# Sums of h inside the first scores, rows of W by another queue, and a shorter last store, in a two-layer graph kernel

## The chip, the core and the metric

The kernel runs on one core of a Trainium2 chip. That core has TensorE (PE in the profile, its weight loads PEld), VectorE (DVE), ScalarE (ACT), GpSimd (POOL) and SyncE (SP), and 16 DMA engines that all queues share. The metric is the device time of one launch in microseconds, lower is better. A measurement is the median of three runs.

## What is computed

Two graph layers over 2708 nodes with 1024 features, in float32. Cut to what matters (biases of layer 0 are zero in the inputs, but are computed):

```python
h = max(layernorm(x), 0)                              # layer 0
f, g = h @ Wf + bf, h @ Wg + bg
scores = where(adj > 0, relu(f @ g.T), -9e15)
x = x + softmax(scores, axis=1) @ (h @ W + bW)

h = max(layernorm(x), 0)                              # layer 1
hw = h @ W1
e = leaky_relu(hw @ a1 + (hw @ a2).T, 0.2)
x = x + relu(softmax(where(adj > 0, e, -9e15), axis=1) @ hw)
```

## The kernel before

**Tiling.** The nodes are cut into five panels of columns (512 to 576 wide) and ten pairs of 128-row tiles, numbered 0 to 9, with one more unit for what is left over. Every large product is done as a Strassen-like scheme: seven products, named M1 to M7, of half-size operands, whose sums and differences VectorE makes before and after. The order of the seven is written out by hand for each stage. The stages of layer 0, panel by panel, are: `project_q` (a small product that prepares the right side of the scores), `scores` (L1360), column maxima and softmax, `aggregate` (L892, attention times h), and `project` (L1210, the result times W). Layer 1 has weights, aggregation (by quarters for panels 1 to 4) and projection only.

**Queues.** Nearly all loads go by SP's queue (`load`, L137), in the order in which the program names them: a load that waits for a free buffer keeps the ones behind it waiting. Nearly all stores go by POOL's queue (`store`, L141). Loads use a pool of 12 buffers called `strm` (`stream`, L128), each of 512 KB; a buffer is free again when its last reader has finished, and where it has been stored from, when the store has landed. All accumulation in PSUM uses a pool of eight banks.

**The list of work.** Work on VectorE, ScalarE and POOL that isn't part of a stage is put on a list, `later`, by `put` (L201), each item with an estimated cost in microseconds and perhaps with a `fetch` of its loads. In the loops of matmuls, `behind(us)` (L214) gives the list a credit, at most twice `us`; `one` (L204) takes an item from the front, after it has issued the fetches of the first `ahead[0]` items. An item with `ready` waits at the front until that is true. `ahead` is 5 until the first scores are over, 2 after that, and 1 in the first aggregation.

**Order on VectorE.** A scheduler may move an instruction ahead of others where it thinks that its operands are there. Where `nc.hold` names an engine, its instructions keep the program's order among themselves. `scores` is held so for VectorE (L1408 to L1485).

**The work around the change.** In panel 0 the sums of h for the first aggregation are made from rows that have been stored to `hg_d`. `sums_h` (L365) puts two items for each pair: `first` after a fetch of two tiles called `hr`, and `second` with three stores. They are needed by M5, M6, M7 and M3 of `aggregate(0, 0)`. It is called at L1714, after `scores`, and `sums_until(3)` runs behind the first product of `project_q(1)`, next to `take_max`, which turns `acc` (the running maximum that `scores` leaves) on PE. The loop over pairs in `scores` is L1410 to L1449; what is left over comes after it (L1451 to L1484).

`prepare_W` (L1312) puts eight items of which each loads two blocks of rows of a W, `w_rows`, by `load_rows` (L529), makes four sums and stores them (`right_of_W`, L1189); for layer 1 it makes eight dot products as well (called junk in the profile, after the output that nobody reads). It is called behind M5 of `aggregate(0, 0)`, whose order is M1, M2, M4, M5, M6, M3, M7. `left` (L921) loads the rows of h, called `hc`, for each product. After M3 `inverse_sums` (L865) adds up columns with four matmuls into two banks, takes reciprocals into `rr`, and `scale` (L982) multiplies with them on POOL behind M7.

At the end, `finish1` (L1794) takes each block of the last projection: relu on ScalarE into `o`, an addition to the residual `x_res` on VectorE, and four stores of 32 rows by POOL's queue.

Of the kernel before, what the change touches and what calls it, by code (L numbers as in the profile page):

```python
# [12 lines left out]
OP = mybir.AluOpType  # L13
# [5 lines left out]
P = 128  # L19
# [38 lines left out]
def kernel(  # L58
# [78 lines left out]
    def load(o, i):  # L137
        for a, b in in_16(o, i):
            tc.keep_in_program_order(nc.sync.dma_start(a, b))
# [61 lines left out]
    def put(us, go, fetch=None, takes_psum=False, ready=None, to=later):  # L201
        to.append([us, fetch, go, takes_psum, ready])
# [11 lines left out]
    def behind(us, psum_free=False):  # L214
# [3 lines left out]
        while spare[0] and not later and lazy and credit[0] > 0:  # L218
            credit[0] -= one(lazy)

    def flush():
        while later:
            one()
# [136 lines left out]
        for m, h in ((M1, ha[0]), (M5, ha[1]), (M2, hb[0]), (M4, hb[1])):  # L360
            store(hg_d[i][:, m, j], h)

    summed = [0]

    def sums_h():  # L365

        def fetch(q, two):
            i, j = group_of[q]
            for m in (M1, M2):
                two.append(stream("hr", (P, 2, W)))  # L370
                load(two[-1], hg_d[i][:, m:m + 2, j])

        def first(q, two):
            (a0, a1), (b0, b1) = ((t[:, 0], t[:, 1]) for t in two)
            add(b1, a1, b1)
            sub(a1, a0, a1)

        def second(q, two):
            (a0, a1), (b0, b1) = ((t[:, 0], t[:, 1]) for t in two)
            sub(a0, b1, a0)  # L380
            sub(b0, b0, a0)
            i, j = group_of[q]
            store(hg_d[i][:, M6:M7 + 1, j], two[0])
            store(hg_d[i][:, M3, j], b0)
            store(hg_d[i][:, M5, j], b1)
            summed[0] += 1
        for q in range(NQ):
            two = []
            put(1.4, lambda q=q, two=two: first(q, two), lambda q=q, two=two: fetch(q, two))
            put(1.4, lambda q=q, two=two: second(q, two))  # L390

    BY_QUARTERS = (M1, M5, M2, M6, M7, M3, M4)
    made_quarters = {}
# [132 lines left out]
            one()  # L526


    def load_rows(w, c, name):  # L529
        t = stream(name)  # L530
        load(t, w[c * P:(c + 1) * P, :])
        return t

    wgT, wfT, M, m_left = [None, None], {}, {}, {}

# [356 lines left out]
    def aggregate(l, p, S, sm, then={}, rate=3.0):  # L892
# [89 lines left out]
        def scale():  # L982
            for e, s, k in ((0, slice(0, w), w), (1, hi, h)):
                nc.gpsimd.tensor_tensor(of(e, s), of(e, s), by(s, k), OP.mult)  # L984

        accumulate(left, right, NQ, h, order, then, evict, "g",
                   {**prepare, M3: lambda: inverse.append(inverse_sums(p, sm)), M7: scale}, rate=rate,
                   by_k=True, more={M2: lambda ps: left_over(ps, 0, lo), M3: lambda ps: left_over(ps, 0, hi),
                                    M4: lambda ps: left_over(ps, 1, lo),
                                    (M7, NQ // 2): lambda: (into_m15(), then.get((M7, "middle"), lambda: None)())})  # L990
        nc.vector.tensor_tensor(of(1, lo), of(1, lo), by(lo, h), OP.mult)
        return [t.rearrange("p (c i) -> p c i", c=NH) for t in G]

# [318 lines left out]
    def prepare_W():  # L1312
        ab, rows = [], {}

        def fetch(l, k):
            if l == 1 and not ab:
                for k2, a in enumerate((a1, a2)):
                    row_to_all(a, wab[k2])
                ab.extend(halves(t) for t in wab)
            rows[l, k] = [load_rows(w_in[l], c, "w_rows") for c in (k, k + NH)]  # L1320

        def go(l, k):
            two = rows.pop((l, k))
            if l == 1:
                for i, c in enumerate((k, k + NH)):
                    for j in range(2):
                        dot(wa[:, j, c:c + 1], halves(two[i]), ab[j])
            right_of_W(l, k, *two)

        for l in range(2):  # L1330
            for k in range(NH):
                put(2.7 if l == 0 else 8.0, lambda l=l, k=k: go(l, k), lambda l=l, k=k: fetch(l, k))
# [27 lines left out]
    def scores(p, B):  # L1360
# [9 lines left out]
            row_on_all(rb, r_d[p], p)  # L1370
        acc = slot("acc")
        S = [None] * NT
        rates = (0.6, 1.0, 0.65, 0.65, 0.65)
        lefts = {}

        def product(q, m, ps, start):
# [33 lines left out]
        for q in range(NQ):  # L1410
            n = P
            make_until(q + 2)
            rate = 1.3 if NQ - 1 not in made else rates[p]
            if q + 2 <= LEFT:
                fetch(q + 2)
            if p in ORDERED and q in (2, 6):
                (copy_residual if q == 2 else bias_residual)(p)
            sa, sb = slot("Sa"), slot("Sb")
            S[pairs[q][0]], S[pairs[q][1]] = sa, sb
            X, Y, Z = (bank(f"s{k}") for k in "xyz")  # L1420
            m1, t = slot("sm1"), slot("st")
            product(q, M1, X, True)
            for s in (lo, hi):
                add(m1[:n, s], X[:n, :h], rb[:n, s])
            if left_over:
                left_over()
            product(q, M6, Z, True)
            add(t[:n, lo], Z[:n, :h], m1[:n, hi])
            behind(rate, True)
            product(q, M5, Y, True)  # L1430
            add(t[:n, hi], Y[:n, :h], m1[:n, hi])
            if q + 1 <= LEFT:
                convert(q + 1, p > 0)
            behind(rate, True)
            product(q, M2, X, False)
            add(sa[:n, lo], X[:n, :h], rb[:n, lo])
            if q + 1 <= LEFT:
                turn(q + 1, 0)
            behind(rate, True)
            product(q, M7, Z, False)  # L1440
            add(sb[:n, hi], Z[:n, :h], t[:n, hi])
            if q + 1 <= LEFT:
                turn(q + 1, 1)
            behind(rate, True)
            product(q, M3, Y, False)
            add(sa[:n, hi], Y[:n, :h], t[:n, lo])
            finish(q, sa, 0)
            behind(2 * rate, True)
            left_over = lambda q=q, sb=sb, Z=Z, m1=m1: last(q, sb, Z, m1)  # L1449

        sm, st = slot("Sa"), slot("Sb")  # L1451
        S[MONO], S[TINY] = sm, st
        X, Y, Z = (bank(f"s{k}") for k in "xyz")
# [252 lines left out]
    for p in range(NP):  # L1706
        got["S"], got["acc"] = scores(p, B)
        generated[p] = NQ + 1
        ahead[0] = 2
        S = got["S"]  # L1710
        hooks = {M1: lambda p=p: take_max(p), M2: lambda p=p: take_softmax(p)}
        if p == 0:
            hooks[M1] = lambda: (take_max(0), sums_until(3))
            sums_h()  # L1714
        if p + 1 < NP:
            B = project_q(p + 1, hooks)
        else:
            nc.hold = ("vector",)
            project(0, p - 1, G.pop(p - 1), finish0(p - 1), hooks)
            nc.hold = ()  # L1720
            scores_before()
        then = {M4: lambda: sums_until(NQ), M5: prepare_W} if p == 0 else {}
        ahead[0] = 1 if p == 0 else 2
        if p == NP - 2:
            then[M2] = lambda: first_masks(NP - 1, 0)
            then[M6] = lambda: first_masks(NP - 1, 1)
            then[M7] = lambda: first_masks(NP - 1, 2)
        spare[0], from_slots[0] = p > 0, p == NP - 1
        G[p] = aggregate(0, p, S, got["sm"], then)
        spare[0] = False  # L1730
        if p == 0:
            flush()
            ahead[0] = 2
            for s in range(1, NP):
                columns_to_row(r_d[s], s, r_[:, first_col[s]:])
            spread_wa()
        if p < NP - 2:
            project(0, p, G.pop(p), finish0(p), {M1: lambda p=p: first_masks(p + 1, 0),
                                                 M5: lambda p=p: first_masks(p + 1, 1),
                                                 M7: lambda p=p: first_masks(p + 1, 2)})  # L1740
# [53 lines left out]
    def finish1(p):  # L1794
        xs = {}

        def start(ts):
            for t in ts:
                if t == TINY:
                    xs[t] = halves_of_tiny("x1_res")  # L1800
                    for e in range(2):
                        for ps, i in by_quarters(x1_d[t], 0, e):
                            load(xs[t][e][ps], i)
                    continue
                xs[t] = row_halves("x1_res", p < NP - 1)
                for e in range(2):
                    load(xs[t][e], x1_d[t][:, e * W:(e + 1) * W])

        def go(t, e, c):
            o = slot("o")[:, :c.shape[1]]  # L1810
            nc.scalar.activation(o, c, AF.Relu)
            add(xs[t][e], xs[t][e], o)
            if t == TINY:
                for ps, to in by_quarters(out, places[t][0][1], e):
                    store(to, xs[t][e][ps])
                return
            for ps, r in places[t]:
                store(out[r:r + ps.stop - ps.start, e * W:(e + 1) * W], xs[t][e][ps])
        return start, None, go
# [54 lines left out]
```

## Time and profile before

| | |
|---|---|
| median of 3 runs | 3078.0 us (3077.63 to 3078.73) |
| the profiled execution, own time | 3082.24 us |
| its span in the profile | 3080.5 us |
| PE busy | 3000.0 us (97%), 14630 matmul instructions |
| VectorE busy | 2046.6 us (66%) |
| ScalarE busy | 551.7 us (18%) |
| POOL busy | 505.5 us (16%) |
| moved by DMA | 766.80 MB, mean 249 GB/s |
| granted clock, mean | 0.99 |

The span runs from the first to the last instruction that was profiled; the execution's own time is 1.7 us longer, and the runs without a profile are a little shorter. A busy PE says that a matmul was under way, not that it ran at full pace: the granted clock beside it tells this. In a line of the timeline come start and length in us, engine, line, operation, output and inputs, and in brackets the idle time before it and what ended it. L45 is a helper through which all of VectorE's and ScalarE's operations go, L139 that of loads and L143 that of stores, so operations are told apart by the names of their tiles.

### The profile page before, as it was taken

Reading aid. Unit: us, or ns where it says so; the run is one execution under the profiler, and the core shown is the slowest. Engines: PE = TensorE matmul, PEld = TensorE weight load, DVE = VectorE, ACT = ScalarE, POOL = GpSimd, SP = SyncE. Lnnn points to the kernel's source line nnn. Section 1 sums busy time; section 2 is a strip of 40 time slices with the busy share of each in tenths; the row PEclk is TensorE's granted clock in tenths of the full one; section 3 lists DMA queues with packets and bytes.
Section 4 is the critical chain, followed back from the end, with each engine's and each line's share of the span. In section 5 each row is a group of like instructions: output and inputs, shape, how many; then the busy total and the mean of one; then the engine's idle time right before and its main releaser. Section 6 shows DMA issues by size and latency. Waiting matters only on the chain.

```text
span 3080.5 us, 41669 instructions
## 1 busy us (share of the span) xinstructions
PE 3000.0 (97%) x14630; PEld 2301.1 (75%) x14630; DVE 2046.6 (66%) x4577; ACT 551.7 (18%) x895; POOL 505.5 (16%) x786
## 2 busy tenths in 40 slices
PE   8998999899999999999999999998999999999998
PEld 4576777657877588885888886784767959879695
DVE  5776693776661586715965276867878768787853
ACT  3420020021110121101211011302222131212200
POOL 1421101310011110214102011131202010020202
PEclk9999999999999999999999999998999999999999
DMA  6988967987565786758967588679757768878786
GB/s 220 304 259 245 302 248 251 314 285 228 177 241 146 226 262 218 247 155 240 284 206 253 165 233 275 230 292 323 250 193 266 260 203 295 289 268 297 266 293 249
DMA packets 447809, 766.80 MB, mean 249 GB/s; under 512 B 175488, under 2 KB 262304, under 8 KB 447568
## 3 DMA queue, kind: packets, MB, share of 16 engines
q1 hardware_dynamic: 392624, 598.30, 60.1%
q0 software_dynamic: 54976, 165.83, 16.1%
q8 instruction: 116, 1.90, 0.2%
q14 instruction: 93, 0.76, 0.1%
HBM read 630.04 MB, written 138.11 MB: 249 GB/s over the span
## 4 chain that ended last, share of the span: by engine, by line
PE 79%; DVE 9%; DMA 5%; issue 5%; SPq 1%; ACT 1%; POOL 0%; POOLq 0%; DVEq 0%; ACTq 0%
PE sz L1385 7%; PE gz L664 6%; PE gx L664 6%; PE gy L664 6%; PE gz L1074 5%; PE pz L1274 5%; PE sx L1385 5%; PE px L1274 4%; PE sy L1385 4%; PE py L1274 4%; PE gx L1074 3%; PE gy L1074 3%; PE gv L664 3%; PE M_ps L577 3%; PE qz L664 3%
## 5 line engine op out<-in xcount | busy, mean ns | idle before, releaser
L1385 PE MATMUL sz<-B,As 128*128 128x288 f32 (+2 forms) x1200 | 292.7, 393 | 3.4 <-DVE st L45 3.3
L1385 PEld LDWEIGHTS sz<-B,As 128*128 128x128 f32 x1200 | 228.1, 191 | 53.0 <-DVE st L45 6.8
L1385 PE MATMUL sx<-B,As 128*128 128x288 f32 (+2 forms) x800 | 203.0, 397 | 13.5 <-DMA As<-hs_d 12.0
L1385 PE MATMUL sy<-B,As 128*128 128x288 f32 (+2 forms) x800 | 199.0, 392 | 0.0
L664 PE MATMUL gz<-Sa,hc 128*128 128x288 f32 (+2 forms) x800 | 190.3, 399 | 6.3 <-DMA hc<-hg_d 6.3
L1385 PEld LDWEIGHTS sx<-B,As 128*128 128x128 f32 x800 | 153.4, 192 | 47.5 <-DMA As<-hs_d 8.0
L664 PEld LDWEIGHTS gz<-Sa,hc 128*128 128x128 f32 x800 | 154.5, 194 | 40.4 <-DMA hc<-hg_d 6.7
L1385 PEld LDWEIGHTS sy<-B,As 128*128 128x128 f32 x800 | 151.7, 190 | 30.6 <-DVE st L45 0.3
L1074 PE MATMUL gz<-quarter,hc 128*128 128x128 f32 (+2 forms) x1344 | 168.8, 279 | 3.8 <-DVE gT L45 3.7
L143 POOL DMA_DIRECT2D out_dram<-x_res x180 | 89.1, 501 | 482.0 <-DVE x_res L45 473.5
L1074 PEld LDWEIGHTS gz<-quarter,hc 128*128 128x128 f32 x1344 | 160.6, 191 | 5.1 <-DVE gT L45 4.6
L1274 PE MATMUL px<-w,gT 128*128 128x512 f32 x320 | 141.2, 593 | 1.5 <-ACT pt L45 1.5
L1274 PE MATMUL py<-w,ps 128*128 128x512 f32 x320 | 142.2, 593 | 0.0
L1274 PE MATMUL pz<-w,ps 128*128 128x512 f32 x320 | 142.1, 594 | 0.0
L143 POOL DMA_DIRECT2D mk_d<-mask x55 | 36.0, 654 | 523.7 <-DVE mask L45 517.3
L1274 PEld LDWEIGHTS pz<-w,ps 128*128 128x128 f32 x320 | 60.2, 190 | 76.2 <-issue 70.5
L1274 PEld LDWEIGHTS py<-w,ps 128*128 128x128 f32 x320 | 60.5, 190 | 75.1 <-issue 72.7
L1274 PEld LDWEIGHTS px<-w,gT 128*128 128x128 f32 x320 | 60.1, 190 | 72.9 <-issue 67.1
L577 PE MATMUL M_ps<-wgT,wfT 128*128 128x512 f32 x256 | 112.5, 595 | 1.6 <-ACT hsT L45 1.6
L664 PE MATMUL gy<-T,hc 128*128 128x288 f32 (+2 forms) x480 | 111.6, 394 | 0.0
L45 ACT ACTIVATE P<-P 128x576 f32<-128x576 f32 (+2 forms) x110 | 72.0, 655 | 207.5 <-DVE P L45 207.4
L984 POOL TENSOR_TENSOR gT<-gT,rr 128x2304 f32<-128x2304 f32 (+5 forms) x12 | 44.4, 3700 | 378.0 <-DVE rr L45 172.7
(382 smaller groups left out, 5892.1 us busy)
## 6 DMA issues: line engine op xcount, KB each, us to landing
hc<-hg_d SPq DMA_DIRECT2D x175, 512.0 KB
As<-hs_d SPq DMA_DIRECT2D x150, 512.0 KB
hc<-hr_d SPq DMA_DIRECT2D x119, 512.0 KB
hc<-hs_d SPq DMA_DIRECT2D x112, 512.0 KB
w<-wt_d SPq DMA_DIRECT2D x96, 512.0 KB
w<-in_L_gnn_W_dram SPq DMA_DIRECT2D x72, 512.0 KB
md<-md_d SPq DMA_DIRECT2D x56, 512.0 KB
adj_i<-in_adj_dram SPq DMA_DIRECT2D x200, 128.0 KB
```

The source lines that it names most:

```text
L45: i = f(*a, **k)
L143: nc.gpsimd.dma_start(a, b)
L577: nc.tensor.matmul(ps, wfT[a][c // NH][:, c % NH, :], wgT[b][c], start=(c == 0), stop=(c == NC - 1))
L664: nc.tensor.matmul(ps[d], left(m, k, d), right(m, k), start=(start and k == 0), stop=(k == K - 1), skip_group_check=True)
L984: nc.gpsimd.tensor_tensor(of(e, s), of(e, s), by(s, k), OP.mult)
L1074: nc.tensor.matmul(ps[:, d], lhs[:, d * P:(d + 1) * P], inner_right(m, n, k), start=(start and k == 0 and d == 0), stop=(k == NK - 1), ski ...
L1274: nc.tensor.matmul(ps, left[i][m][:, k, :], w_[k], start=(start and k == 0), stop=(k == NH - 1), skip_group_check=True)
L1385: nc.tensor.matmul(ps[:n, :h], lefts[q][:, i % 2, c, :n], B[m][c // 2][:, c % 2, :h], start=(start and c == 0), stop=(c == NH - 1), skip_g ...
```

## The change

Five edits in one. (1) `sums_h` is called at pair 8 of the scores of panel 0; its items' VectorE operations are held in order; a flag stops them from the end of the loop over pairs until `take_max` is done; the credit of panel 0 goes from 0.6 to 0.8. (2) In the first aggregation `prepare_W` is called behind M4 instead of M5. (3) The rows of W are loaded by ScalarE's queue, in order there. (4) The inverse sums of that aggregation are made in the middle of M7 instead of behind M3. (5) In the last panel of layer 1 relu and addition are one VectorE operation, and the results of the last two tiles are stored by ScalarE's queue, every second store of the very last block by SP's.

```diff
+    def held(f, *a):
+        was, nc.hold = nc.hold, ("vector",)
+        r = f(*a)
+        nc.hold = was
+        return r
+
...
-    summed = [0]
+    summed, sums_may = [0], [True]
...
-            put(1.4, lambda q=q, two=two: first(q, two), lambda q=q, two=two: fetch(q, two))
-            put(1.4, lambda q=q, two=two: second(q, two))
+            put(1.4, lambda q=q, two=two: held(first, q, two), lambda q=q, two=two: fetch(q, two), ready=lambda: sums_may[0])
+            put(1.4, lambda q=q, two=two: held(second, q, two), ready=lambda: sums_may[0])
...
-    def load_rows(w, c, name):
+    def load_rows(w, c, name, by=load):
         t = stream(name)
-        load(t, w[c * P:(c + 1) * P, :])
+        by(t, w[c * P:(c + 1) * P, :])
         return t
+
+    def by_scalar(o, i):
+        tc.keep_in_program_order(nc.scalar.dma_start(o, i))
...
+        def invert():
+            inverse.append(inverse_sums(p, sm))
+
         accumulate(left, right, NQ, h, order, then, evict, "g",
-                   {**prepare, M3: lambda: inverse.append(inverse_sums(p, sm)), M7: scale}, rate=rate,
+                   {**prepare, M7: scale, **({} if first else {M3: invert})}, rate=rate,
                    by_k=True, more={M2: lambda ps: left_over(ps, 0, lo), M3: lambda ps: left_over(ps, 0, hi),
                                     M4: lambda ps: left_over(ps, 1, lo),
-                                    (M7, NQ // 2): lambda: (into_m15(), then.get((M7, "middle"), lambda: None)())})
+                                    (M7, NQ // 2): lambda: (first and invert(), into_m15(), then.get((M7, "middle"), lambda: None)())})
...
-            rows[l, k] = [load_rows(w_in[l], c, "w_rows") for c in (k, k + NH)]
+            rows[l, k] = [load_rows(w_in[l], c, "w_rows", by_scalar) for c in (k, k + NH)]
...
-        rates = (0.6, 1.0, 0.65, 0.65, 0.65)
+        rates = (0.8, 1.0, 0.65, 0.65, 0.65)
...
+            if p == 0 and q == NQ - 2:
+                sums_h()
...
+        sums_may[0] = False
         sm, st = slot("Sa"), slot("Sb")
...
-            hooks[M1] = lambda: (take_max(0), sums_until(3))
-            sums_h()
+            hooks[M1] = lambda: (held(take_max, 0), sums_may.__setitem__(0, True), sums_until(3))
...
-        then = {M4: lambda: sums_until(NQ), M5: prepare_W} if p == 0 else {}
+        then = {M4: lambda: (sums_until(NQ), prepare_W())} if p == 0 else {}
...
-            o = slot("o")[:, :c.shape[1]]
-            nc.scalar.activation(o, c, AF.Relu)
-            add(xs[t][e], xs[t][e], o)
+            if p == NP - 1:
+                nc.vector.scalar_tensor_tensor(xs[t][e], c, 0.0, xs[t][e], op0=OP.max, op1=OP.add)
+                if t in full(p)[F // 2:]:
+                    end = t == full(p)[-1] and e == 0
+                    for i, (ps, r) in enumerate(places[t]):
+                        by = nc.sync if end and i % 2 else nc.scalar
+                        tc.keep_in_program_order(by.dma_start(out[r:r + ps.stop - ps.start, e * W:(e + 1) * W], xs[t][e][ps]))
+                    return
+            else:
+                o = slot("o")[:, :c.shape[1]]
+                nc.scalar.activation(o, c, AF.Relu)
+                add(xs[t][e], xs[t][e], o)
```

## The prediction

> **What bounds the kernel now.** I read the page first: its engine table says PE is busy 3000.0 of 3080.5 us. So time can come only from about 80 us in which PE stands still, from PE running slowly, and from the ends. The view of what PE waited for sorts the idle part:
>
> ```profile
> PE sx L1385 <- DMA As<-hs_d: 12.0, 3, 7.5
> PE mx_ps L856 <- DVE mx L45: 8.3, 1, 8.3
> PE gz L664 <- DMA hc<-hg_d: 6.3, 1, 6.3
> PE mx_ps L856 <- DVE acc L45: 5.9, 1, 5.9
> PE sum_ps L871 <- DVE gT L45: 4.5, 1, 4.5
> ```
>
> Columns: waiting group, released by, total us, times, longest. The first row (at the start of the scores) and the second (layer 1) lie outside the change. The other three lie inside it, at 389, 543 and 579 us. The timeline of PE there:
>
> ```profile
> 395.11 1.33 PE L856 MATMUL mx_ps<-ident,acc 128*128 128x128 f32 x5 [5.90 <-DVE acc L45]
> 396.23 8.88 PE L664 MATMUL qx<-hT,md 128*128 128x288 f32 x32
> 413.54 7.92 PE L664 MATMUL qz<-hT,md 128*128 128x288 f32 x32
> ...
> 549.79 6.79 PE L664 MATMUL gz<-Sa,hc 128*128 128x288 f32 x16 [6.26 <-DMA hc<-hg_d]
> 574.66 4.15 PE L664 MATMUL gy<-Sb,hc 128*128 128x288 f32 x16
> 583.31 2.30 PE L871 MATMUL sum_ps<-sm,ones 128*128 128x288 f32 x4 [4.50 <-DVE gT L45]
> 585.41 13.73 PE L664 MATMUL gz<-Sa,hc 128*128 128x288 f32 x48
> ```
>
> The same 32 matmuls take 8.88 us after a gap and 7.92 later; 16 take 6.79 after a gap and 4.15 otherwise. So a gap costs more than its idle time. The table by windows shows why: the granted clock (third number from the right) is 0.50 after the gap.
>
> ```profile
> 549.80:552.00 2.20, 2.20 (x5) 1.63 (x6) 2.13 (x9) 0.00 (x0) 0.54 (x1) 0.50 1.02 417
> 552.00:554.00 2.00, 2.00 (x6) 1.43 (x5) 1.97 (x6) 0.00 (x0) 0.20 (x1) 0.50 1.03 420
> ```
>
> Full price of each gap: at 389, 5.9 idle + 1.0 (8.88 - 7.92) + about 0.5 on the slow transposes = **7.4**. At 543, 6.3 + 2.6 (6.79 - 4.15) = **8.9**. At 579, 4.5 + 1.9 (48 matmuls at the pace of 15.68 us for 64 are 11.8, not 13.7) + 0.6 for the four of sum_ps = **7.0**. Together 23.3 us.
>
> The causes, from the timelines of VectorE and SP and from the program's last line:
>
> ```profile
> 389.03 0.69 DVE L45 TENSOR_TENSOR hr<-hr 128x512 f32<-128x512 f32 x1 [7.86 <-DMA hr<-hg_d]
> ...
> 332.98 4.89 SPq L139 DMA_DIRECT2D As<-hs_d  x8
> 337.97 0.65 SPq L139 DMA_DIRECT2D As<-hsl_d  x1
> 341.38 0.32 SPq L139 DMA_DIRECT2D As<-hs_d  x1
> 354.02 14.88 SPq L139 DMA_DIRECT2D hr<-hg_d  x8
> ...
> L1869 POOLq DRAIN  x3: 46/102/5932, 3073.7 to 3080.2; - x3
> ```
>
> At 381 VectorE stood 7.86 us before a sum of h whose load was late, and the final `acc` behind it kept PE waiting: gap one. At 543, SP had waited for stores of W (17.1 us in 525 to 552, by its wait view) with loads of `hc` queued behind: gap two. At 579 the junk products of W delayed the eviction of M3, which frees the banks of sum_ps: gap three. At the end POOL's drain runs 5.9 us from 3073.7, past the last landing (stores of `out` land in 2.0 us, from 3074.4 to 3076.4): it, not the data, sets the end at 3080.5.
>
> **What the Trainium skill says.** "TensorE: Matmul & The Clock Gate", What's actually happening: after an idle window of about 3.4 us the array's clock is halved, until about 3.4 us of work; the trace agrees (0.50 after gaps of 4.5 us and more). "DMA: Bandwidth & Descriptors", Issuing engines are not separate DMA queues: DMAs of ScalarE and SP share the same 16 engines, so another issuer saves only issue time. So W on ScalarE's queue brings no bandwidth; it brings what stands in SP's order. No DMA of ScalarE is in this trace. Same page, Specifications: first byte about 1 us by GpSimd's path, 0.6 by SP's and ScalarE's; no row here shows the two side by side. "SBUF — State Buffer", SBUF: two separate sides: GpSimd and a VectorE operation with two SBUF inputs exclude each other for a whole instruction; the trace agrees, a subtraction beside the 5.30 us POOL multiply at 589 took 5.42 instead of 0.69.
>
> **The change, part by part.**
>
> *Sums of h (L365, L1410 to L1449, L1714).* They enter the queue of work at pair 8 (of 0 to 9) instead of after the scores, with VectorE's order fixed. Credit per pair is 7 x 0.8 = 5.6 us, at 1.4 an item four items; with the credit saved up (1.6) nine items go out before the flag stops them: four pairs summed and half a fifth. One item is two operations at a pace of 0.60 to 0.69, 1.25 us. VectorE is busy 8.65 of 13.6 us per pair (windows of 300 to 340); plus 4 x 1.25 = 13.65, just full. PE tolerates a lag of some 3.3 us (M6's result is needed two products of 1.94 later, less the add), and my schedule by hand lags 2.5. So the operations themselves cost nothing; without that slack each costs 1.25 us. The final `acc` then comes at about 385, before 389: **-7.4**.
>
> The loads cost something. `ahead` is 5 there, so the first item fetches three pairs, six tiles of 512 KB, ahead of pair 8's `As` for M5. The stream pool has 12 buffers, and in the lines above SP stopped at 337.97 with exactly 12 taken (two masks, nine As, hsl) until M7's tile of pair 7 came free at 341.2. With six hr in the pool: As for M5 of pair 8 is issued near 337.5 behind 4.25 MB, which at 390 GB/s lands near 346 (needed 347.0); As for M7 at 347 when M1's tile frees (lands 350.7, needed 350.9); As for M1 of pair 9 only at 354.8, when M7's tile or the first stored hr frees, and is needed at 354.8. Landing takes 2.9 to 6.7 us (minimum and median of hr), so PE stands about 3.5 us, with 1.5 for the slow clock: **+5**. Bounds: 0, if hr frees sooner (its stores land in 6.7 median), and +15 if three loads are that late. hT, loaded at 342 before, moves to about 368 to 378, needed at 384: in time by a little. Net of this part **-2.4**.
>
> *W's rows (L529, L1320, L1722).* 16 loads leave SP's order. They are moved past SP's hc loads; behind them on ScalarE stands nothing until `carry` at 594 (its timeline is empty from 487). The work, 16 loads, 24 stores on POOL (0.54 each to issue) and on VectorE 64 operations of 0.69 with 32 reads of 0.08, 46.7 us, starts a product (19.4 us) earlier, where VectorE is busy 6.7 of 50 us and DMA 0.59 (window 480 to 530). W ends near 565 instead of 597. Gap two goes, -8.9; but eight buffers hold W while M5 runs, and 8 MB of loads and stores fall on 20 us that also need 2.5 MB of hc, so I leave 2 us: **-6.9**. Bounds -8.9 and, if the gap returns whole, 0.
>
> *Inverse sums (L987) from M3's end into M7's middle.* M3's eviction is prompt then, and banks are free 11.6 us later. Same four matmuls. The two reciprocals (3.75 us) end about 16 us into M7, POOL's multiply (5.3) at about 21.5, and the projection that reads it starts at 24.8: hidden with 3 us to spare; without that, up to +3. **-6.8** of 7.0.
>
> *Tail (L1809).* Relu goes into the add: one ScalarE step less on the chain (0.63 and its hops, 0.66); the fused operation reads as the add did, 0.69 (junk products of that form: 0.68). Four stores at 0.49 on POOL become two each on ScalarE and SP; ScalarE's price is unknown, between SP's 0.32 and POOL's 0.49, I take 0.35. So: last matmul 3070.07, results 3071.5, issued 3072.3, landed 3074.3 to 3075.3 (2.0 as POOL's stores, 2.9 as the fastest hr), closing 0.84 as after POOL's drain: 3075.1 to 3076.1 against 3080.5, **-5** (bounds -3.5 and -6). The big term is the drain: POOL's last store is then near 3049.
>
> Sum: -2.4 - 6.9 - 6.8 - 5 = **-21.1**. The profiled execution took 3082.2 (span 3080.5), so 3061.1; the median of the runs, 3078.0, is 4.2 below it: **3057**.
>
> **Rivals.**
> *Clean*: no new wait. -7.4 - 8.9 - 7.0 - 5 = -28: 3050. For it: SP stood 8 us ahead at pair 8. Against: the 12 buffers.
> *W's gap returns*: hc shares buffers and engines with W whoever issues, so M5 or M6 waits as before: -21.1 + 6.9 and 2 more of lateness = -12: 3066. For it: DMA is at 1.03 in that gap.
> *Even*: scores lose 15 and W half: +7.6 - 3.5 - 3 - 5 = -4: 3074.
> *Slower*: the pool of 12 runs dry in pairs 8 and 9. SP in its order then waits for stores of hr, 9.6 us at the longest already ("SPq L139 <- DMA hg_d<-hr", 24.3 us in 345 to 400). Four As or hT loads in turn late by 9.6 and 2.6 of slow clock are 49; less 7.4, 6.9, 6.8 and 5 is +23: 3101. It decides from three such waits on (37, +11).
> The change not doing what it says: the scheduler may reorder work that isn't fixed; but the loads and held sums are fixed, so I give that nothing of its own.
>
> **Numbers.** Forecast 0.45, clean 0.10, W's gap 0.16, even 0.11, slower 0.18. A measurement tells about 0.2% from no change, 6 us. So faster 0.71, same 0.11, slower 0.18. Range 3046 to 3078: clean to even, with the slower case left out; the forecast's own is 3050 to 3065.
>
> **What would show it.** Right: no wait of mx_ps for acc, of gz for hc, of sum_ps for gT; clock 1.00 from 390 to 610; hr from about 347; short waits of sx for As at 345 to 360; ACT issues of w_rows from about 490; drain of POOL short. Wrong: waits of PE for As over 10 us in the scores, an hc wait in M5, or a projection that waits for POOL's multiply.

## The result, and the profile after

The changed kernel takes 3074.4 us (median of 20 runs, 3069.8 to 3082.4) against 3081.3 us for the kernel before (20 runs beside them, 3076.9 to 3086.9). The ratio is 0.9981, with an interval of 0.9975 to 0.9987: a gain of some 5.8 us, where 21 had been forecast (3057 against the 3078.0 of the kernel before that the forecast started from).

The engine table of the page says that PE does the same work in a shorter span of 3069.2 us (before 3080.5):

```profile
PE 2999.9 (98%) x14630; PEld 2298.9 (75%) x14630; DVE 2042.9 (67%) x4577; ACT 546.1 (18%) x887; POOL 496.0 (16%) x770
```

The spans differ by 11.2 us, and that is not the gain. The matmuls are the same in number and, but for the four of the inverse sums, in order, so the start of the same matmul in both traces cuts the execution into stages that can be compared; a wait ahead of the first matmul of a stage counts in the stage before it. Of the 11.2 us, 6.3 lie ahead of pair 8 of the first scores, where the change alters nothing: pair 8 starts anywhere from 334.9 to 345 us in the profiles of this study. The stages from there on give the other 4.9:

| stage (us, profiles of before and after) | before | after | difference | predicted |
|---|---|---|---|---|
| scores, pairs 8 and 9 | 27.2 | 40.4 | +13.3 | |
| scores, what is left over | 12.9 | 15.8 | +2.9 | |
| `project_q(1)`, with the turn of `acc`, to the start of the aggregation | 63.3 | 55.7 | -7.6 | |
| *sums of h together* | | | **+8.6** | -2.4 |
| M1, M2, M4 of the aggregation | 63.9 | 63.9 | 0.0 | |
| M5 | 19.4 | 25.3 | +5.9 | |
| M6 | 28.6 | 19.4 | -9.2 | |
| *W's rows together* | | | **-3.3** | -6.9 |
| M3 up to the start of M7 | 29.0 | 22.2 | -6.8 | |
| M7 | 25.9 | 26.7 | +0.8 | |
| *inverse sums together* | | | **-6.0** | -6.8 |
| first projection to the last matmul | 2458.7 | 2460.1 | +1.4 | 0 |
| *last matmul to the end* | 10.4 | 4.8 | **-5.6** | -5 |

The view of what PE waited for has none of the three old rows (mx_ps for `acc`, gz for `hc`, sum_ps for gT). New ones stand in it (waiting group, released by, total us, times, longest):

```profile
PE sx L1397 <- DMA As<-hs_d: 14.6, 3, 6.4
PE gy L673 <- DMA hc<-hg_d: 3.9, 1, 3.9
PE sx L1475 <- DMA As<-hsl_d: 3.6, 1, 3.6
PE sz L1397 <- DMA As<-hs_d: 1.3, 1, 1.3
```

Only one of the three in the first row lies here, the other two at other stages. The timeline of PE places them (start, length, engine, line, operation, tiles, and in brackets the idle time ahead):

```profile
346.01 2.18 PE L1397 MATMUL sz<-B,As 128*128 128x288 f32 x8 [1.29 <-DMA As<-hs_d]
348.02 2.10 PE L1397 MATMUL sy<-B,As 128*128 128x288 f32 x8
355.30 4.21 PE L1397 MATMUL sx<-B,As 128*128 128x288 f32 x8 [5.17 <-DMA As<-hs_d]
...
375.30 4.21 PE L1475 MATMUL sx<-B,As 128*128 128x288 f32 x8 [3.60 <-DMA As<-hsl_d]
...
398.90 0.71 PE L865 MATMUL mx_ps<-ident,acc 128*128 128x128 f32 x5
...
530.29 5.83 PE L673 MATMUL gy<-T,hc 128*128 128x288 f32 x16 [3.91 <-DMA hc<-hg_d]
535.97 19.56 PE L673 MATMUL gz<-Sa,hc 128*128 128x288 f32 x80
...
589.24 1.13 PE L880 MATMUL sum_ps<-sm,ones 128*128 128x288 f32 x4
```

The turn of `acc` (mx_ps), M6 (the 80 gz at 535.97) and the inverse sums (sum_ps) run without a gap. But PE stands for 1.29, 5.17 and 3.60 us in the scores, at M7 of pair 8, at M1 of pair 9 and at the first product of what is left over, and for 3.91 us in M5. After the long gaps eight matmuls of the scores take 4.21 us instead of 2.10: the table by windows (window, its length, busy us of PE, PEld, DVE, ACT and POOL, then granted clock, DMA share, GB/s) shows the clock at half, and what the DMA engines did just before.

```profile
338.60:340.80 2.20, 2.20 (x11) 1.73 (x10) 1.79 (x3) 0.00 (x0) 0.00 (x0) 1.00 0.30 50
347.40:349.00 1.60, 1.60 (x9) 1.23 (x8) 1.06 (x4) 0.00 (x0) 0.00 (x0) 1.00 0.46 157
...
355.30:357.30 2.00, 2.00 (x4) 1.51 (x5) 0.00 (x0) 0.00 (x0) 0.00 (x0) 0.50 1.03 399
```

Shortly before PE starves, the DMA engines move little: 50 GB/s in 338.6 to 340.8 and 157 in 347.4 to 349, at a share of 0.30 and 0.46. The loads that PE then waits for had not been issued yet. SP's timeline shows it:

```profile
323.30 7.38 SPq L139 DMA_DIRECT2D hr<-hg_d  x6
331.17 0.33 SPq L139 DMA_DIRECT2D As<-hs_d  x1
335.05 4.24 SPq L139 DMA_DIRECT2D hr<-hg_d  x2
340.87 0.33 SPq L139 DMA_DIRECT2D As<-hs_d  x1
347.88 0.94 SPq L139 DMA_DIRECT2D hr<-hg_d  x2
348.91 1.68 SPq L139 DMA_DIRECT2D As<-hs_d  x3
...
363.97 3.40 SPq L139 DMA_DIRECT2D hr<-hg_d  x2
367.85 0.52 SPq L139 DMA_DIRECT2D As<-hsl_d  x1
```

Six `hr` go out ahead of the `As` for M5 of pair 8 (331.17), and from then on SP issues an `As` only when buffers have come free for it and for the `hr` ahead of it. The last one, hsl, whose load was issued at 338 before the change, now stands behind 14 loads of `hr` and goes out at 367.85; PE starts on it at 375.30. What SP waited for, in 322 to 372 and in 470 to 556:

```profile
SPq L139 <- DMA hg_d<-hr: 18.4, 3, 8.9
...
SPq L139 <- DMA wt_d<-w_rows: 36.2, 6, 10.2
```

In the scores it was above all the stores of finished sums, whose buffers it needed; in the aggregation the stores of W, although no load of W's rows is in SP's queue any more. At the end, the long drain of POOL (8.27 us here) begins at 3045.1 and is over 11 us before the last matmul ends (POOL's queue at the program's last line; times in ns, then first and last start):

```profile
L1892 POOLq DRAIN  x1: 8267/8267/8267, 3045.1 to 3045.1; - x1
```

### The profile page after: what moved, and what is told of

The parts are those of the page before. It is cut to its first block, busy times and chain, and to the rows that moved or that the text cites. A ratio compares the mean times of both kernels' runs of the same rounds, so it can differ in the third digit from the quotient of the medians.

```text
span 3069.2 us, 41688 instructions
## 1 busy us (share of the span) xinstructions
PE 2999.9 (98%) x14630; PEld 2298.9 (75%) x14630; DVE 2042.9 (67%) x4577; ACT 546.1 (18%) x887; POOL 496.0 (16%) x770
## 4 chain that ended last, share of the span: by engine, by line
PE 75%; DVE 9%; issue 7%; DMA 6%; POOL 1%; SPq 1%; ACT 1%; POOLq 0%; DVEq 0%; ACTq 0%
PE gy L673 7%; PE sz L1397 7%; PE gz L673 7%; PE gx L673 6%; PE gz L1086 5%; PE sx L1397 4%; PE sy L1397 4%; PE px L1286 4%; PE pz L1286 4%; PE py L1286 3%; PE gx L1086 3%; PE gy L1086 3%; PE gv L673 3%; PE M_ps L586 3%; PE qz L673 2%
## 5 line engine op out<-in xcount | busy, mean ns | idle before, releaser
L1397 PEld LDWEIGHTS sx<-B,As 128*128 128x128 f32 x800 | 153.5, 193 | 51.2 <-DMA As<-hs_d 12.9
L143 POOL DMA_DIRECT2D out_dram<-x_res x164 | 80.9, 500 | 467.2 <-DVE x_res L45 456.6
L673 PEld LDWEIGHTS gy<-T,hc 128*128 128x128 f32 x480 | 92.2, 192 | 24.4 <-DMA hc<-hg_d 4.4
```

What stands on the lines that cost most here:

```text
L143: nc.gpsimd.dma_start(a, b)
L673: nc.tensor.matmul(ps[d], left(m, k, d), right(m, k), start=(start and k == 0), stop=(k == K - 1), skip_group_check=True)
L1397: nc.tensor.matmul(ps[:n, :h], lefts[q][:, i % 2, c, :n], B[m][c // 2][:, c % 2, :h], start=(start and c == 0), stop=(c == NH - 1), skip_g ...
```

## The experiments

All ratios are to the kernel before, in runs on the same chip; 0.001 is 3.1 us. Stage times are from one profile each and are differences to the profile of before.

### The sums of h

**Fewer loads ahead** (`e1_ahead2`): the changed kernel with a look ahead of two items, one pair of rows, from the call on.

```diff
             if p == 0 and q == NQ - 2:
+                ahead[0] = 2
                 sums_h()
```

> The changed kernel with one line more: the list of work looks 2 items ahead instead of 5 while the sums run inside the scores, so that at most two pairs of hr are held at once instead of three or four. Theory (the 12 buffers): the three waits of PE for As and hsl in pairs 8, 9 and the remainder (10.1 us idle, about 6 at half clock) shrink to under 3 us together, and the kernel gains 10 to 16 us on the changed one: about 3060 where that has 3074. Rival (VectorE is full, its lag holds PE): the loads come as late as before for PE's purposes, the gain is under 3 us. A third possibility: with so short a look ahead VectorE itself waits for hr in its fixed order, and the loss stays though its name changes.

0.9945 (0.9932 to 0.9957), 3067.3 us. Pairs 8 and 9 cost +4.0 instead of +13.3, what is left over +1.8; everything after is as in the changed kernel. One wait is left in this place on PE's timeline:

```profile
372.69 2.90 PE L1476 MATMUL sx<-B,As 128*128 128x288 f32 x8 [3.80 <-DMA As<-hsl_d]
```

The smaller look ahead gives back 10.4 of the 16.2 us that the scores had lost. It is hsl, last in the queue, that still comes late.

**This part undone** (`e2_sums_old`): the changed kernel with `sums_h` after the scores again, in the old order of VectorE and with the old credit.

```diff
-        rates = (0.8, 1.0, 0.65, 0.65, 0.65)
+        rates = (0.6, 1.0, 0.65, 0.65, 0.65)
...
-            if p == 0 and q == NQ - 2:
-                sums_h()
...
-            hooks[M1] = lambda: (held(take_max, 0), sums_may.__setitem__(0, True), sums_until(3))
+            hooks[M1] = lambda: (take_max(0), sums_until(3))
+            sums_h()
```

> The changed kernel with the sums of h put back behind the scores, not held, rate 0.6; W, inverse sums and tail stay changed. From the traces the sums part cost 16.2 us in pairs 8 to the remainder and returned 7.6 at the wait of mx_ps for acc. Theory: this kernel is 8 to 9 us faster than the changed one (about 3066), with the 5.9 us wait of mx_ps for acc back and no wait for As after pair 8. Rival (the sums part gained as forecast and the loss lies elsewhere): 2 to 8 us slower than the changed one.

0.9959 (0.9947 to 0.9971), 3072.6 us: better than with the part in. The scores are back at the old time to 0.1 us, the wait for `acc` is back with 5.45 us. M5, M6 and M3 are as in the changed kernel.

**This part alone** (`e13_sums_only`): the kernel before, with nothing but part 1 of the change.

> The kernel before with the sums part alone. Theory: 16 us lost in pairs 8 to the remainder, 7.5 returned at the turn of acc: 7 to 10 us slower than before. Rival (its loss needs the other edits): no slower than before.

1.0038 (1.0025 to 1.0050), about 12 us slower. +12.7 and +1.6 in the scores, -7.6 in `project_q(1)`: nothing after that differs by more than 1 us. These stages add up to +6.6 only; the profiled execution is the fastest of the five (3087.6 to 3093.2). The part by itself is a loss.

**Half the bytes** (`e7_hr_half`): the changed kernel, whose `hr` loads bring only the first of the two blocks of rows, so that sums and differences are made of other data; buffers, number of loads and stores are the same.

```diff
-                load(two[-1], hg_d[i][:, m:m + 2, j])
+                load(two[-1][:, 0], hg_d[i][:, m, j])
...
-            add(b1, a1, b1)
-            sub(a1, a0, a1)
+            add(b1, a0, b0)
+            sub(a1, a0, b0)
```

> The changed kernel with each hr load cut to half its bytes; it leaves out the second half of the rows of h, and the sums are made from the first half twice, with the same operations, buffers, stores and order. Theory (buffers: SP waits for a free one of the 12): the waits of PE for As and hsl in pair 8 to the remainder stay, at 7 us or more of the 10.1. Rival (bandwidth: three pairs of hr stand ahead of As on the DMA engines): they fall to half or less, 5 us.

0.9961 (0.9948 to 0.9974). The scores lose 8.4 us instead of 16.2; PE's timeline has two of the three waits left, both shorter:

```profile
356.26 3.90 PE L1397 MATMUL sx<-B,As 128*128 128x288 f32 x8 [2.98 <-DMA As<-hs_d]
...
375.02 2.21 PE L1475 MATMUL sx<-B,As 128*128 128x288 f32 x8 [3.10 <-DMA As<-hsl_d]
```

Of the 10.1 us of standing 6.1 stay, between what the two theories had said. So it is neither buffers alone nor bytes alone. With the number of buffers and the order as they were, half of the loss stays; the other half goes with the bytes. How that half divides isn't shown: smaller loads land sooner, and free their buffers sooner too, and one of the two waits left happens not to be followed by the slow clock (2.21 us for eight matmuls).

**At most three pairs** (`e6_three`): `e1_ahead2`, and no more than three pairs of sums until the scores are over.

```diff
-            put(1.4, ..., ready=lambda: sums_may[0])
+            put(1.4, ..., ready=lambda q=q: sums_may[0] and (q < 3 or sums_after[0]))
```

> The changed kernel with a look ahead of 2 while the sums run in the scores, and with at most three pairs of sums there, so that hr tiles of the fourth and fifth pair do not hold buffers when hsl is to be loaded. Theory: the wait for hsl that stood in the run with a look ahead of 2 (3.8 us, 1.8 of slow clock) goes, no wait of PE longer than 1 us is left between pair 8 and the turn of acc, and it is 4 to 6 us faster than that run: about 3062 where the changed kernel has 3074. Rival: the remaining sums land behind acc or in the aggregation, where they cost as much.

0.9936 (0.9924 to 0.9948), 3060.9 us. The scores lose 1.4 us, in one short wait, and `project_q(1)` keeps its gain of 7.6:

```profile
355.58 2.21 PE L1397 MATMUL sy<-B,As 128*128 128x288 f32 x8 [1.16 <-DMA As<-hs_d]
```

That is the part as it was meant: -6.2 instead of +8.6. With only this mended, the whole change brings 0.64%, some 20 us.

### The rows of W

**This part undone** (`e3_w_old`): the changed kernel with W behind M5 again and loaded by SP.

```diff
-            rows[l, k] = [load_rows(w_in[l], c, "w_rows", by_scalar) for c in (k, k + NH)]
+            rows[l, k] = [load_rows(w_in[l], c, "w_rows") for c in (k, k + NH)]
...
-        then = {M4: lambda: (sums_until(NQ), prepare_W())} if p == 0 else {}
+        then = {M4: lambda: sums_until(NQ), M5: prepare_W} if p == 0 else {}
```

> The changed kernel with the rows of W on SP's queue again and put behind M5; sums, inverse sums and tail stay changed. By the traces the W part gained 9.2 us at M6 and lost 5.9 in M5. Theory: 3 to 4 us slower than the changed one (about 3078), the wait for hc back in M6 and gone from M5. Rival (the hc wait in M5 is due to the sums, which run on later, not to W): the wait in M5 stays and the loss is 9.

0.9999 (0.9991 to 1.0007): without this part the change gains nothing. M5 is at its old time, and gz in M6 waits for `hc` again (6.48 us).

**Another queue only** (`e9_w_queue`): the changed kernel with W behind M5 again, but still loaded by ScalarE's queue.

```diff
-        then = {M4: lambda: (sums_until(NQ), prepare_W())} if p == 0 else {}
+        then = {M4: lambda: sums_until(NQ), M5: prepare_W} if p == 0 else {}
```

> The changed kernel with the rows of W put behind M5 again as before, but still by ScalarE's queue: the queue alone. Theory (hc waits for buffers that hold rows of W until their stores land, whoever issues): the wait for hc moves from M5 back to M6, M5 to M3 cost about 5.9 us more than free of waits, as in the changed kernel, against 9 with SP's queue: within 2 us of the changed kernel. Rival (it is SP's order that made it wait): no hc wait, 5 us faster than the changed kernel.

1.0012 (1.0005 to 1.0020), slower than before and some 9.5 us slower than the changed kernel, where the theory had said within 2. The two waits on PE's timeline:

```profile
556.12 6.77 PE L673 MATMUL gz<-Sa,hc 128*128 128x288 f32 x16 [4.11 <-DMA hc<-hg_d]
...
635.95 9.09 PE L1286 MATMUL py<-w,ps 128*128 128x512 f32 x16 [10.40 <-DMA w<-wt_d]
```

The queue by itself shortens the wait for `hc` (4.1 us here, 5.9 to 6.9 in the six profiles with W's rows behind M5 on SP's queue) and doesn't remove it. With the earlier start as well, M6 is free of it, and 3.9 us of it stand in M5 instead. A second wait is new here, at the first projection.

**W's work spread out** (`e10_w_spread`): the changed kernel with other estimates for W's items, so that fewer are taken at once.

```diff
-                put(2.7 if l == 0 else 8.0, lambda l=l, k=k: go(l, k), lambda l=l, k=k: fetch(l, k))
+                put(5.0 if l == 0 else 7.0, lambda l=l, k=k: go(l, k), lambda l=l, k=k: fetch(l, k))
```

> The changed kernel with the items of W spread out: their estimated costs 5.0 (layer 0) and 7.0 (layer 1) instead of 2.7 and 8.0, so that two of them fall into M5 instead of four. Theory (buffers): the wait of PE for hc in M5 (3.9 us, 5.9 with the slow clock) goes, 4 to 6 us faster than the changed kernel. Rival: the wait moves to M6 or M3, or the end of W runs into the projection; no gain.

0.9991 (0.9982 to 1.0000). The wait in M5 is gone (M5 +0.0, M6 still -9.2), and SP's waits in the changed kernel name the stores of W's rows; together this speaks for W's buffers as what held back `hc`, though fewer rows of W at once are also fewer bytes beside `hc`, which no run separates. But the projection gives all of that back and more, +13.1:

```profile
627.86 9.14 PE L1286 MATMUL py<-w,ps 128*128 128x512 f32 x16 [10.49 <-DMA w<-wt_d]
```

SP's timeline tells why:

```profile
583.46 8.24 SPq L139 DMA_DIRECT2D w<-in_L_gnn_W_dram  x4
591.75 19.32 SPq L139 DMA_DIRECT2D x_res<-in_x_dram  x32
...
623.03 1.83 SPq L139 DMA_DIRECT2D w<-wt_d  x4
```

The `w` that the third product of the projection needs is issued at 623.0, after 32 loads of x_res and 16 of the adjacency, some 31 us of SP's time from 591.8 on. The head of this chain waits for buffers that W's rows still hold, as SP's waits in 575 to 630 tell:

```profile
SPq L139 <- DMA wt_d<-w_rows: 28.2, 5, 17.8
```

Where this chain is late by some microseconds, PE stops at the projection; where PE comes there sooner and the chain doesn't, it stops too (`e14_invert_only` and `e12_best` below).

**This part alone** (`e18_w_only`): the kernel before, with parts 2 and 3 of the change.

> The kernel before with the part of W alone (ScalarE's queue, behind M4). Theory from the stages: M5 +5.9, M6 -9.2, M7's start about -5 (VectorE is no longer behind with W when M3's evictions come), so 7 to 9 us faster at the projection and as much at the end, since SP's chain starts earlier too. Rival (without the inverse sums moved, the four matmuls still wait for banks): 3 us faster.

0.9961 (0.9948 to 0.9973): some 12 us, twice what the whole change brings. M5 costs +5.9, M6 -9.2, as in the changed kernel. And M3 to M7 gets 5.8 faster and M7 itself 1.9, although the inverse sums are where they were. PE's timeline:

```profile
524.70 5.84 PE L667 MATMUL gy<-T,hc 128*128 128x288 f32 x16 [3.98 <-DMA hc<-hg_d]
...
572.01 1.13 PE L874 MATMUL sum_ps<-sm,ones 128*128 128x288 f32 x4
```

sum_ps doesn't wait for gT any more, because the junk products of W that delayed gT are over by then: the last one begins at 556.5, before M3's evictions into gT from 569.3 on. (In the kernel before they run until 584.) M5 to M7 give -11.0 here and -9.3 in the changed kernel: once W is moved, part 4 brings nothing more, in one profile each.

### The inverse sums

**This part alone** (`e14_invert_only`): the kernel before, with part 4.

> The kernel before with the inverse sums alone moved into the middle of M7. Theory: 4.5 us of idle and 2.5 of slow clock go at the start of M7, 0.8 come back in it: 5 to 7 us faster than before, with no new wait. Rival (VectorE is still behind with W, so its late evictions hold M7 elsewhere): under 2 us.

0.9999 (0.9989 to 1.0008). M7 starts 6.8 us sooner after M3, as forecast, and the first projection gives all of it back (+8.1 within its first 64 matmuls, +11.7 until the last matmul). PE's wait, and SP's load of `w` for it:

```profile
622.36 9.14 PE L1277 MATMUL py<-w,ps 128*128 128x512 f32 x16 [5.88 <-DVE bn L45]
...
615.94 5.23 SPq L139 DMA_DIRECT2D w<-wt_d  x4
```

The view names VectorE. But the load went out on SP only at 615.94, at the end of the same chain as above, so the name left two explanations open.

**The w first** (`e16_invert_w_first`): the same, with the `w` of the third product loaded ahead of x_res and the adjacency.

```diff
-        ws = {m: load_W(l, m) for m in order[:2]}
+        ws = {m: load_W(l, m) for m in order[:3 if l == 0 and p == 0 else 2]}
```

> The kernel before with the inverse sums moved into M7, and with the loads of w for the projection's third product (M5) issued ahead of the 32 loads of the residual and 16 of masks, for layer 0's panel 0 only. In the run with the inverse sums alone the 6.8 us gained in M7 came back as a wait of 5.9 us (and slow clock) at that product. Theory (SP's chain of loads sets when the projection can go on): the wait is gone and 5 to 7 us are kept against before. Rival (the residual's sums on POOL's queue are late for VectorE, which holds the banks): the wait stays.

0.9992 (0.9985 to 0.9999): 2.5 us are kept, not the 5 to 7 of the theory. The wait at py is gone, so the late load of `w` had been its cause, and not VectorE. The next product then waits for its own `w`:

```profile
633.24 8.80 PE L1277 MATMUL pz<-w,ps 128*128 128x512 f32 x16 [1.91 <-DMA w<-wt_d]
```

At 64 matmuls into the projection +3.8 is lost instead of +8.1. SP has the same list of loads to get through either way; the order among them moves the wait by one product and halves it.

### The last stores

**This part alone** (`e4_tail_only`): the kernel before, with part 5.

> The kernel before with the tail alone: relu and addition in one operation, stores of the last two tiles by ScalarE's queue and SP's. Theory: 5 to 6 us faster than before (10.4 us from the last matmul to the end become 4.8), all of it after the last matmul. Rival (the tail gains only the ScalarE step and the issue time): 2 us.

0.9978 (0.9970 to 0.9985), 6.8 us (4.6 to 9.3). From the last matmul to the end 4.8 us instead of 10.4, in this kernel as in the changed one; nothing else differs by more than the runs do.

### Toward a better version

**Both repairs** (`e12_best`): `e6_three`, with W's items at 4.0 and 6.0.

> The changed kernel with a look ahead of 2 and three pairs of sums in the scores, and with the items of W at 4.0 and 6.0: three of layer 0 instead of four and the first of layer 1 ahead of M5's last loads, and the end of W no later. Theory: no wait of PE over 1.2 us from pair 8 to the projection, the 10 us wait for w in the projection of the spread run absent: 4 to 6 us faster than the run with three pairs, near 3056 where before has 3082. Rival (the end of W is late for SP's chain of loads again): the gain in M5 is lost in the projection.

0.9944 (0.9932 to 0.9957). The loss in the scores is 1.3 us, the wait in M5 is gone, and the projection takes the gain of M5 back with a wait of 5.39 us for `w`. Against `e6_three` nothing is gained.

**A look ahead of one** (`e15_best_ahead1`): the same with `ahead[0] = 1`.

> The same with a look ahead of 1. Theory (buffers): within 2 us of it, the last wait of 1.2 us in pair 9 gone. Rival (each load of hr now comes with its use, and VectorE in its fixed order waits for it): PE waits for VectorE in pairs 8 and 9, over 4 us slower.

0.9944 (0.9932 to 0.9957). The scores now lose nothing at all (0.0 in both stages), and `project_q(1)` still gains 7.6. The projection waits 7.58 us for `w`, so this too is given back.

**Both repairs and the w first** (`e17_best_w_first`): `e12_best` with the edit of `e16_invert_w_first`.

> The run with three pairs and W at 4.0 and 6.0, with the same loads of w first. Theory: its wait of 5.4 us at the projection (7.5 with the slow clock) goes: 5 to 8 us faster than it, near 3054 where before has 3081. Rival: a wait for the residual takes its place, under 2 us.

0.9925 (0.9913 to 0.9938), 3059.8 us: the lowest ratio of all, some 23 us below the kernel before and some 17 below the changed one. Its interval overlaps with those of `e12_best` and `e6_three`, so that it is better than these isn't shown. The wait for `w` is 1.76 us. Its profile still has +8.5 from the first projection on: 2.0 in the projection, and part of the rest at the start of panel 1.

## Why the prediction was wrong

The four parts alone measured +0.38% (sums), -0.39% (W), -0.01% (inverse sums) and -0.22% (tail): -0.24% together (about 0.2 either way), -0.19% in one. The forecast of -21.1 us and the -4.9 of the stages differ by 16.2: 11.0 of it in the sums of h, 3.6 in W's rows, 0.8 in the inverse sums and 1.4 in stages that the change doesn't touch, less 0.6 at the end.

**Sums of h: the term that failed is the "+5" for late loads.** It measured 16.2. The mechanism is the one that the text named, and its issue times were right: with the 6.3 us by which this execution is early, the three loads were to go out at 331.2, 340.7 and 348.5, and went out at 331.17, 340.87 and 348.91. Four things in the term were too small:
- The stall at M1 of pair 9 was put at 3.5, near the minimum (2.9) of the landing times of `hr`; PE could start 6.4 us after the issue of the load, near their median (6.7), and stood 5.17.
- M7's load was to land 0.2 us in time; it took 5.1 us where 3.7 had been allowed: 1.29.
- hsl was left out. It is the load that the change delays most, from 338 to 368, since a queue kept in order hands a delay on to its last entry: 3.60.
- The slow clock was put at 1.5 us for one gap; two long gaps and a short one cost 6.1 (16.2 less 10.1 of standing).

The other terms of this part held. Nine items went out before the flag stopped them (18 sums on VectorE before the turn of `acc`), none of them delayed PE, and the gap at the turn gave 7.6 for the 7.4 forecast. The bound of +15 for "three loads that late" was drawn in the text, and three were late, with hsl in the place of M5's load: the value taken lay too near the lower end. `e6_three` confirms that this term was most of the miss: with the loads in time the edited stages give -21.1 and the runs some 20 us. That the stages hit the forecast so exactly is in part luck, since sums of -6.2 for -2.4 make up for W's -3.4 for -6.9.

**W's rows and inverse sums: two terms for one wait.** The text gave -6.9 to W and -6.8 to the inverse sums as if they were independent. `e18_w_only` shows that W alone removes the wait of sum_ps too (the text itself had named W's junk products as its cause), and `e14_invert_only` that moving the sums brings nothing by itself. The stage table's -6.0 can therefore not be credited to part 4. Of W's own term, -8.9 for M6 measured -9.2; the 2 us left back for M5 measured 5.9. The cause was foreseen ("eight buffers hold W while M5 runs"), and `e10_w_spread` agrees with it. (The text counts 24 stores of W; there are 32, since eight more go out of `wT`. No number of the sum rests on it.)

**What the text didn't contain: the chain of loads ahead of the first projection.** It checked whether POOL's multiply would be ready there, and in the changed kernel it was. It didn't ask whether the `w` would be. In the changed kernel this happens to be in time, with `w` issued at 608.4 for a projection from 604.3 on. In `e9_w_queue`, `e10_w_spread`, `e12_best`, `e14_invert_only` and `e15_best_ahead1` it isn't, and 5.4 to 10.5 us go there. With only the loads of the scores mended (`e6_three`) it is in time as well, so it was no part of the miss; it takes back what is gained beyond that (`e12_best`, `e15_best_ahead1`).

**Tail: -5, measured -5.6.** That the drain was the big term is read from the traces and not tested apart: in the kernel before, the last store landed at 3075.8 (1.9 us after the start of its issue) and the drain ended at 3079.6, 3.8 us later. A store issued by ScalarE took 0.43 us (median of ten) for the 0.35 assumed.

**The rivals.** The time is that of *Even* (3074), and so are its reasons in kind: the scores lose 16.2 (it said 15) and W brings about half. It had 0.11; the slower case, with four stalls of 9.6, was not reached, since no stall was longer than 5.2. Of the 17 us between the forecast and *Even*, 10 were one choice, one late load or three; and that SP was already at the end of its 12 buffers, which the text had read in the trace of before, spoke for three.

**What stays open.** From the first projection to the last matmul the nine profiles without a long wait for `w` differ from that of before by +0.5 to +6.5 us, in stages that no edit touches. Part of it lies at the start of panel 1's scores, where PE waits for VectorE: 1.6 us for `st` instead of 0.34 in the changed kernel and the seven others that have part 4 and no wait for `w` over 2 us, and 2.20 for `sm` in `e17_best_w_first`. Why VectorE comes later there no run shows. `e2_sums_old` gains less (12.6 us) than W and tail alone would add up to (18.8), and such a loss is in its profile (+6.5 from the projection on); the intervals, 2.3 to 3.9 us on either side, don't exclude chance.

## What to carry to other kernels

When loads are moved forward in a queue that is kept in order and shares a pool of buffers with others, follow every load behind them to the last one: ask when its buffer comes free, and price the wait at the median of the landing times at least, with the slow clock after it. Look no further ahead than the work will be used: here a look ahead of 2 instead of 5 was worth 11 us, where the whole change had brought 6. When several waits are removed one behind the other, check whether one cause makes two of them, and which load, not only which result, the next stage needs first.

## What the runs showed of the hardware

- How long a gap slows PE isn't set by its length alone. In `e7_hr_half` 2.98 us of standing was followed by 3.90 us for eight matmuls, and 3.10 us by 2.21, full speed (granted clock 0.51 and 1.00 in the 2 us behind them); in `e16_invert_w_first` even 1.91 us was followed by 0.50, and the product took 1.8 us more than its 7.0, while 1.76 us in `e17_best_w_first` cost nothing. The Trainium skill, "TensorE: Matmul & The Clock Gate", What's actually happening, gives about 3.4 us as the idle window that halves the clock and calls the window free-running. A free-running window would fit two gaps of nearly equal length that end differently; that 2.98 and 1.91 us were enough lies below the page's figure.
- A drain of POOL's queue after its last stores took 5.92 to 5.94 us in the five profiles with the old tail and 8.05 to 8.41 in the twelve with the new one. In the changed kernel it begins 19 us before the last matmul ends and delays nothing; in the kernel before, where POOL's stores come last, it ends 3.8 us after they have landed.
- A DMA issued by ScalarE held its sequencer for 0.33 us (16 of W's rows, minimum and median 334 ns, one of 912), against 0.54 for POOL's stores of W.
